# Layer 0's and layer 2's feed forward taken batch by batch, with the normalizations around them, layer 1's k and v projections, and the delta rule's output normalization in its last slots

## The chip, the cores and the metric

The kernel runs on one core of one Trainium2 chip. A core has five engines with instruction queues of their own: PE (matrix multiply, with PEld for its weight loads), DVE (vector), ACT (activation functions and scaled copies), POOL (general vector work), and SP (which here only issues DMAs). Each queue is executed in order; engines wait for each other through semaphores. The metric is the device time of one execution in microseconds; the figure shown is the median of several executions.

## What is computed

A stack of four transformer-like layers on an input x of 4 batches of 1024 tokens with 128 channels, all in float32. Each layer adds two terms to x, both computed from a layer normalization of x. The parts that matter here:

```python
x = x + deltanet(layernorm(x))        # layer 0: a recurrence over tokens; its output o is normalized:
                                      #   (o - mean) / sqrt(var + 1e-5) * ln_w + ln_b
x = x + quantum_ffn(layernorm(x))     # layer 0: h = xn @ W1 + b1
                                      #   q = h + c * sin(theta + 0.1 * h);  relu(q) @ W2 + b2
x = x + ttt(layernorm(x))             # layer 1: k, v = xn @ W_KV, then a sequential scan over tokens
x = x + experts(layernorm(x))
x = x + attention(layernorm(x))       # layer 2
x = x + rwkv_ffn(layernorm(x))        # layer 2: r = sigmoid(xr @ W_r); out = r * (relu(xk @ W_k)^2 @ W_v)
                                      #   xr, xk mix each token with the token before it
x = x + attention(layernorm(x))       # layer 3
x = x + routed_experts(layernorm(x))
```

## The kernel before

x stays on the chip as 32 tiles of 128 tokens (`self.x`), batch b being tiles 8b to 8b+7. A normalization (`layernorm`, which calls `ln_batch` for each of the four batches, lines 92 to 144) takes eight `bn_stats` on DVE (L108), a few small DVE operations (L110 to L114), a square root on ACT (L116), a reciprocal (L117) and a product (L127); then it scales eight tiles, half on ACT (L134) and half on POOL (L132), transposes them on PE (L138) through PSUM, and copies the result into `self.xnT` with ACT (L144). Its pools are opened and closed in `layernorm` itself.

The program is written against a tile framework. Outside of a `manual_schedule` block the framework decides the order of the instructions on each engine: earlier ones in the text have priority, a later one whose inputs are there may pass. Inside a `manual_schedule` block the order of the text holds on each engine. A pool that is opened after another was closed may lie in the same memory, and its first writers then wait for the last readers there. Each pool has a number of buffers (`bufs`) per tile name[...].

**Layer 0's delta rule** (`l0_attn`, lines 174 to 512). 1024 tokens in NS = 32 chunks of 32. The main loop (L441) runs over slots from -LAG-1 to NS+3, LAG being 12, in an order written by hand. In slot c the loop does, among others:

- the state step of chunk c: `up` and `op` (L388), `ux` and `uP` on ACT (L453, L455), `sp` (L464), the state copies (L472), `oT` (L484), `o` (L501) and its store to `od` in DRAM (L502);
- `gram(c + LAG)` (L304, L328): a score whose blocks go to DRAM (`ld`, L331); after every fourth chunk they are read back as `L` (L334);
- `solve(n, i)` (L346, L349), DVE alone: a block of four chunks is solved column by column in eight parts over four slots, two parts a slot, and part 7 stores the result `T` to `td` in DRAM (L351);
- `fetch(c + 2)` (L357): reads chunk c+2's part of T back as `tb`; `apply(c + 1)` (L376) multiplies with it;
- `attend(c + 2)`: a score on PE (L304) and the masked copy `mt` on DVE (L393), which stands between the slot's two solve parts; it shares the PSUM tile `wide` with `gram`;
- `flip(c + LAG + 1)` (L310 to L321): two POOL products and four transposes.

Block n is solved in slots 4n-7 to 4n-4; its first chunk is fetched in slot 4n-2 and applied in slot 4n-1. The output normalization of block n (four chunks) is spread over slots: `reload` in 4n+4 (one DMA from `od`, L408, and a POOL add of the bias, L409), `moments` in 4n+6 (four `bn_stats` and `bn_aggr`, L417 and L418, on DVE), `root` and `norm` in 4n+7 (L423 on ACT; L428, L430 and L432 on DVE).

**Layer 0's feed forward** (`l0_ffn`). After `layernorm()`, 8 chunks of 512 tokens with 4 hidden blocks each: a matmul into `hp` (L559), `r` on ACT (L563), two DVE operations that take off full turns (L530, L531), the sine on ACT (L566), a DVE product (L567), a Relu on ACT (L568); then 16 matmuls into `op` (L573), a POOL add of b2 (L149) and a DVE add to x (L153). The sine of the angles (L549) is one small operation ahead of the chunks.

**Layer 1's attention** (`l1_attn`). After `layernorm()`, for each chunk of 512 tokens a k and a v matmul into `pp` (L619, a PSUM pool of four buffers), copied with a stride of four elements into `kT` by DVE (L621) and into `vT` by ACT (L623). Then `l1_rounds`, a manually ordered sequential scan that begins with chunk 0 of all four batches.

**Layer 2's feed forward** (`l2_ffn`). After `layernorm()`, per batch: two mixes (ACT L1403, DVE L1404), two halves with `kp` (L1408), Relu (L1412), a POOL square (L1413), `rp` (L1417), `vp` (L1422), Sigmoid (L1426), a DVE product (L1427), a POOL add to x (L1429). **Layer 3's attention** (`l3_attn`) begins with `layernorm()` and then `attention`, whose setup (L1092 to L1116) and first projections (L1147) precede its manually ordered main loop.

Of the kernel before, what the change touches and what calls it, by code (L numbers as in the profile page):

```python
# [9 lines left out]
F32 = mybir.dt.float32  # L10
AF = mybir.ActivationFunctionType
# [16 lines left out]
class Net:  # L28
# [71 lines left out]
    def ln_batch(self, pool, ps, b, twice=None):  # L100

# [25 lines left out]
        nc.vector.scalar_tensor_tensor(nm, s, -0.5, rs, ALU.mult, ALU.mult)  # L127
        xn = pool.tile([P, TPB, D], F32, tag="xn", name="xn")
# [39 lines left out]
    def l0_attn(self):  # L168
# [9 lines left out]
        NS, LAG = SEQ // C, 12  # L178
# [3 lines left out]
        with ExitStack() as c_:  # L182
# [222 lines left out]
            def reload(n):  # L405

                o = two.tile([P, NB, D], F32, tag="on", name="on")
                nc.sync.dma_start(o, od[:, n * P : (n + 1) * P, :].rearrange("b p d -> p b d"))  # L408
                nc.gpsimd.tensor_add(of(n), of(n), ln_b.unsqueeze(1).to_broadcast([P, NB, D]))  # L409
                outs[n] = [o]  # L410

            def moments(n):
                o = outs[n][0]
                mv = two.tile([P, NB, 2], F32, tag="mv", name="mv")
# [26 lines left out]
            for slot in range(-LAG - 1, NS + 4):  # L441
                c, part = slot, (slot + 7) % 4
                n = (slot + 7) // 4
# [16 lines left out]
                for i in every(7):  # L460
                    root(i)
# [45 lines left out]
                for i in every(4):  # L507
                    reload(i)
                for i in every(6):
                    moments(i)  # L510
                for i in every(7):
                    norm(i)
# [20 lines left out]
    def l0_ffn(self):  # L533
# [4 lines left out]
        self.layernorm()  # L538
        with tc.tile_pool(name="f0", bufs=3) as two, tc.tile_pool(name="f0c", bufs=1) as one, tc.tile_pool(
            name="f0h", bufs=4, space=PSUM  # L540
        ) as ph, tc.tile_pool(name="f0o", bufs=2, space=PSUM) as po:
            ang = one.tile([P, 3, NF], F32, tag="ang", name="ang")
            nc.vector.tensor_scalar_mul(ang[:, 1, :], f["th"], INV)
            nc.vector.tensor_scalar(ang[:, 2, :], f["th"], INV, 0.25, ALU.mult, ALU.add)
            nc.vector.scalar_tensor_tensor(ang[:, 0, :], f["b1"], 0.1, f["th"], ALU.mult, ALU.add)
            nc.vector.tensor_scalar_mul(ang[:, 0, :], ang[:, 0, :], INV)
            self.turns(one, ang, [P, 3, NF])
            sc = one.tile([P, 2, NF], F32, tag="sc", name="sc")
            nc.scalar.activation(sc, ang[:, 1:3, :], AF.Sin, scale=TWO_PI)  # L549
            co = one.tile([P, NF], F32, tag="co", name="co")  # L550
            nc.vector.tensor_mul(co, sc[:, 1, :], f["wr"])
            nc.vector.tensor_mul(sc[:, 0, :], sc[:, 0, :], f["wi"])
            nc.vector.tensor_add(co, co, sc[:, 0, :])
            nc.vector.scalar_tensor_tensor(co, co, 0.1, f["wi"], ALU.mult, ALU.mult)
            for n in range(NB * SEQ // 512):
# [21 lines left out]
                self.add_four(4 * n, op)  # L577

# [16 lines left out]
    def l1_attn(self):  # L595
# [12 lines left out]
        self.layernorm()  # L608
        with ExitStack() as c_:
            one = c_.enter_context(tc.tile_pool(name="l1c", bufs=1))  # L610
            two = c_.enter_context(tc.tile_pool(name="l1", bufs=2))
            kT = one.tile([P, SEQ, NB], F32, tag="kT", name="kT")
            vT = one.tile([P, SEQ, NB], F32, tag="vT", name="vT")
            with tc.tile_pool(name="l1p", bufs=4, space=PSUM) as ps:
                for n in range(NB * SEQ // 512):
                    b, s = n // 2, (n % 2) * 512
                    for dst, cols in ((kT, slice(0, 128)), (vT, slice(128, 256))):
                        pp = ps.tile([P, 512], F32, tag="pp", name="pp")
                        nc.tensor.matmul(pp, lhsT=wkv[:, cols], rhs=self.tok(4 * n, 512), start=True, stop=True)  # L619
                        if dst is kT:  # L620
                            nc.vector.tensor_copy(dst[:, s : s + 512, b], pp)  # L621
                        else:
# [1084 lines left out]
```

## Time and profile before

| | us |
|---|---|
| median of 3 runs (2716.39 to 2722.8) | 2716.49 |
| the profiled execution, its own time | 2722.97 |
| its span, first to last instruction | 2721.3 |

| engine | busy us | share of the span | instructions |
|---|---|---|---|
| PE | 2465.4 | 91% | 19913 |
| DVE | 1809.7 | 67% | 3643 |
| ACT | 1484.3 | 55% | 3315 |
| POOL | 292.8 | 11% | 526 |

The stages that the change touches, by the times at which their instructions stand in the trace:

| stretch | us from the span's start |
|---|---|
| delta rule: end of the setup, first solve, slot 0, slot 31 | 49.2, 70.0, 112.1, 363.7 |
| last output normalization done, layer 0's first sqrt of the feed forward's normalization | 380.4 |
| first and last work of the eight chunks | 397.5, 474.1 |
| layer 1's normalization done | 490.9 |
| k and v done, layer 1's rounds begin | 508.9 |
| last copy of layer 2's attention | 1507.1 |
| layer 2's feed forward: first mix, last add | 1529.6, 1565.5 |
| layer 3's normalization done, its first projection | 1585.9 |
| first score of layer 3's attention | 1603.8 |

How to read the views: a timeline line has the start and the length in microseconds, the engine, the line of the kernel, the operation, output tile, `<-`, input tiles, shapes, how many were merged, and in brackets how long the engine had been idle and what ended the wait. "SPq" and the like are queue instructions such as DMA issues. A busy share is an average; what bounds a stretch is seen in who waits there.

### The profile page before, as it was taken

Reading aid. Unit: us, or ns where it says so; the run is one execution under the profiler, and the core shown is the slowest. Engines: PE = TensorE matmul, PEld = TensorE weight load, DVE = VectorE, ACT = ScalarE, POOL = GpSimd, SP = SyncE. Lnnn points to the kernel's source line nnn. Section 1 sums busy time; section 2 is a strip of 40 time slices with the busy share of each in tenths; the row PEclk is TensorE's granted clock in tenths of the full one; section 3 lists DMA queues with packets and bytes.
Section 4 is the critical chain, followed back from the end, with each engine's and each line's share of the span. In section 5 each row is a group of like instructions: output and inputs, shape, how many; then the busy total and the mean of one; then the engine's idle time right before and its main releaser. Section 6 shows DMA issues by size and latency. Waiting matters only on the chain.

```text
span 2721.3 us, 50960 instructions
## 1 busy us (share of the span) xinstructions
PE 2465.4 (91%) x19913; PEld 1232.3 (45%) x19913; DVE 1809.7 (67%) x3643; ACT 1484.3 (55%) x3315; POOL 292.8 (11%) x526
## 2 busy tenths in 40 slices
PE   5688758899997989999999669999999999999968
PEld 4455536699995333333333423333333333333356
DVE  5899748566664856776772457767767777777143
ACT  4465457655554424665566523666566666666632
POOL 6112020100002520000000440000000000000011
PEclk8688769899997958999999757999999999999968
DMA  2333220000000001001000000000000000000000
GB/s 47 70 80 78 61 72 1 1 1 1 1 2 2 1 9 17 14 14 18 14 14 5 5 4 6 12 8 9 9 8 8 12 8 9 10 8 8 4 17 17
DMA packets 116718, 46.65 MB, mean 17 GB/s; under 512 B 88473, under 2 KB 111097, under 8 KB 116474
## 3 DMA queue, kind: packets, MB, share of 16 engines
q1 hardware_dynamic: 116474, 43.35, 8.1%
q8 instruction: 159, 2.61, 0.4%
q14 instruction: 85, 0.70, 0.1%
HBM read 17.04 MB, written 12.98 MB: 11 GB/s over the span
## 4 chain that ended last, share of the span: by engine, by line
PE 62%; DVE 4%; ACT 1%; POOL 1%; issue 1%; DMA 0%; SPq 0%; POOLq 0%; DVEq 0%; ACTq 0%
PE pb L1232 31%; PE po L1254 16%; PE pa L1207 5%; PE ep L1026 2%; PE pp L1147 1%; PE tp L138 1%; PE gp L959 1%; PE pv L1128 1%; DVE st L108 1%; PE rp L1625 1%; DVE bm L1219 0%; DVE x L1035 0%; PE bp L1015 0%; PE pr L1480 0%; PE hp L648 0%
## 5 line engine op out<-in xcount | busy, mean ns | idle before, releaser
L1236 ACT ACTIVATE es<-pb 128x512 f32<-128x512 f32 x1536 | 836.2, 594 | 560.0 <-PE pb L1232 405.6
L1232 PE MATMUL pb<-q,k 32*128 32x512 f32 x3072 | 957.8, 642 | 0.9 <-ACT es L1236 0.9
L1207 PE MATMUL pa<-k,q 32*128 32x512 f32 x3072 | 913.4, 682 | 17.2 <-DMA q<-q 15.9
L1219 DVE TENSOR_REDUCE bm<-pa 128x2 f32<-128x1024 f32 x512 | 626.0, 1225 | 276.5 <-PE pb L1232 169.9
L1254 PE MATMUL po<-es,v 128*32 128x256 f32 (+1 forms) x5760 | 480.0, 405 | 0.0
L1232 PEld LDWEIGHTS pb<-q,k 32*128 32x128 f32 x3072 | 314.8, 184 | 348.2 <-ACT es L1236 189.6
L1215 DVE TENSOR_REDUCE bm<-pa 128x16 f32<-128x1024 f32 x256 | 312.8, 1222 | 107.7 <-PE pb L1232 60.7
L1254 PEld LDWEIGHTS po<-es,v 128*32 128x32 f32 x5760 | 114.1, 108 | 543.0 <-issue 510.5
L1207 PEld LDWEIGHTS pa<-k,q 32*128 32x128 f32 x3072 | 254.1, 194 | 94.8 <-DVE bm L1219 50.6
L132 POOL TENSOR_SCALAR xn<-x,rs,nm 128x128 f32<-128x128 f32 x112 | 48.8, 449 | 1259.1 <-DMA oc<-oT 992.5
L138 PE MATMUL tp<-ident,xn 128*128 128x128 f32 x224 | 52.6, 401 | 63.0 <-ACT xn L134 50.3
L346 DVE TENSOR_TENSOR pr<-T,L 128x31 f32<-128x31 f32 (+15 forms) x248 | 90.9, 367 | 27.8 <-DMA L<-ld 20.8
L1261 DVE COPY oT<-po 128x512 f32<-128x512 f32 x48 | 32.7, 682 | 109.1 <-PE po L1254 109.1
L349 DVE TENSOR_TENSOR T<-T,pr 128x31 f32<-128x31 f32 (+15 forms) x248 | 92.8, 374 | 8.5
L304 PE MATMUL wide<-bt,kt 32*128 32x128 f32 x512 | 32.0, 381 | 48.6 <-DVE mt L393 33.3
L138 PEld LDWEIGHTS tp<-ident,xn 128*128 128x128 f32 x224 | 37.7, 196 | 81.2 <-ACT xn L134 45.5
L766 ACT ACTIVATE w<-tr,half 128x128 f32<-128x128 f32 x128 | 47.1, 368 | 48.8 <-PE tr L764 46.7
L741 ACT ACTIVATE a<-hp,wb 128x128 f32<-128x128 f32 x128 | 47.1, 368 | 41.1 <-PE hp L737 40.1
L1026 PE MATMUL ep<-L_ffn_expert_w,xnT 128*128 128x512 f32 x128 | 66.1, 649 | 3.3 <-DVE x L1035 3.0
L464 PE MATMUL sp<-ux,kn 128*128 128x256 f32 x128 | 50.5, 532 | 17.8 <-ACT ux L453 17.7
L749 DVE TENSOR_TENSOR dlt<-gr,mask 128x128 f32<-128x128 f32 x96 | 28.0, 292 | 48.6 <-PE gr L747 48.3
L1035 DVE SCALAR_TENSOR_TENSOR x<-ep,g,x 128x128 f32<-128x128 f32 x160 | 49.5, 342 | 13.1 <-ACT sc L1033 8.1
(462 smaller groups left out, 3466.1 us busy)
## 6 DMA issues: line engine op xcount, KB each, us to landing
ld<-kk SPq DMA_DIRECT2D x128, 32.0 KB
L<-ld SPq DMA_DIRECT2D x8, 512.0 KB
td<-T SPq DMA_DIRECT2D x8, 512.0 KB
tb<-td SPq DMA_DIRECT2D x128, 32.0 KB
md<-nt SPq DMA_DIRECT2D x192, 2.0 KB
q<-md SPq DMA_DIRECT2D x192, 2.0 KB
x<-in_L_attn_x_dram SPq DMA_DIRECT2D x4, 512.0 KB
od<-o SPq DMA_DIRECT2D x32, 64.0 KB
```

Source lines behind the costliest of these rows:

```text
L138: nc.tensor.transpose(tp[:, i, :], xn[:, 4 * n + i, :], self.ident)
L346: nc.vector.tensor_mul(pv, T[:, 0 : j + 1, j : j + 1].to_broadcast(sh), L[:, j : j + 1, j + 1 :].to_broadcast(sh))
L349: nc.vector.tensor_sub(T[:, 0 : j + 1, j + 1 :], T[:, 0 : j + 1, j + 1 :], pv)
L464: mm(sp[:, g].rearrange("p a b -> p (a b)"), lhsT=kns[c % len(kns)][:, 4 * g : 4 * g + 4, :].rearrange("p a b -> p (a b)"), rhs=ux[:, g].r ...
L1026: nc.tensor.matmul(ep.rearrange("p a b -> p (a b)"), lhsT=self.tok(t), rhs=ew[:, 4 * h : 4 * h + 4, :].rearrange("p a b -> p (a b)"), star ...
L1035: nc.vector.scalar_tensor_tensor(xs, eps[e // 4][:, e % 4, :], g[:, e : e + 1], xs, ALU.mult, ALU.add)
L1207: nc.tensor.matmul(pa[:, j % 2, :], lhsT=st["q"][r, i * P : (i + 1) * P], rhs=st["k"][r, n * 512 : (n + 1) * 512], start=True, stop=True,)
L1215: nc.vector.tensor_reduce(out[:, :, 1:9], pa.rearrange("p j (c s) -> p j c s", c=8), axis=AX.X, op=ALU.max)
L1219: nc.vector.tensor_reduce(out[:, :, n : n + 1], pa, axis=AX.X, op=ALU.max)
L1232: nc.tensor.matmul(pb, lhsT=st["k"][r, kc * P : (kc + 1) * P], rhs=st["q"][r, n * 512 : (n + 1) * 512], start=True, stop=True,)
L1236: nc.scalar.activation(es[turn][:, j, :], pb, AF.Exp, scale=scale)
L1254: nc.tensor.matmul(po[r, cols], lhsT=vring[b % 2][:, kc, 4 * g + j, :], rhs=es[:, j, cols], start=kc == 0, stop=True, skip_group_check=True,)
```

## The change

1. `ln_batch` is cut in two: `ln_moments(pool, b)` (up to `rs` and `nm`) and `ln_scale(pool, ps, b, by)` (scaling, transposes, copies). Nothing else of it changes.
2. Delta rule: LAG is 11 instead of 12, the loop runs over 47 slots instead of 49 (-12 to 34), and the solve of block n stands in slots 4n-6 to 4n-3. The output normalization of blocks 0 to 6 is reloaded in slots 23 to 29, one block a slot, that of block 7 in slot 32; moments follow one slot later, root and norm two slots later. The tiles `on` and `mv` have three buffers instead of two.
3. Layer 0's feed forward: all pools are open together; the normalization runs batch by batch between the chunks, and a function handed in by layer 1 (`behind`) normalizes layer 1's input and projects k and v for batches 0 and 1 after chunk 4 and for batches 2 and 3 after chunk 7. The angles' operations stand after the first two batches' scaling. `hp` has three PSUM buffers instead of four, the normalization's `tp` two instead of four, `pp` one instead of four. Layer 1 calls layer 0's feed forward.
4. Layer 2's feed forward: all four moments first, then batch by batch with the scaling one batch ahead; layer 3's normalization of batches 0 and 1 after batch 2, that of batches 2 and 3 after batch 3; `l3_attn` no longer calls `layernorm`. The sigmoid is computed as (tanh(z/2) + 1)/2, the half going into a copy of W_v made once.

```diff
-        NS, LAG = SEQ // C, 12
+        NS, LAG = SEQ // C, 11
...
-            for slot in range(-LAG - 1, NS + 4):
-                c, part = slot, (slot + 7) % 4
-                n = (slot + 7) // 4
+            reloads = [NS - TPB - 1 + i for i in range(TPB - 1)] + [NS]
+            for slot in range(-LAG - 1, NS + 3):
+                c, part = slot, (slot + 6) % 4
+                n = (slot + 6) // 4
...
-                for i in every(7):
-                    root(i)
+                if slot - 2 in reloads:
+                    root(reloads.index(slot - 2))
...
-                for i in every(4):
-                    reload(i)
-                for i in every(6):
-                    moments(i)
-                for i in every(7):
-                    norm(i)
+                if slot in reloads:
+                    reload(reloads.index(slot))
+                if slot - 1 in reloads:
+                    moments(reloads.index(slot - 1))
+                if slot - 2 in reloads:
+                    norm(reloads.index(slot - 2))
```

```diff
-    def l0_ffn(self):
+    def l0_ffn(self, behind):
...
-        self.layernorm()
-        with tc.tile_pool(name="f0", bufs=3) as two, tc.tile_pool(name="f0c", bufs=1) as one, tc.tile_pool(
-            name="f0h", bufs=4, space=PSUM
-        ) as ph, tc.tile_pool(name="f0o", bufs=2, space=PSUM) as po:
+        with ExitStack() as c_:
+            ln = c_.enter_context(tc.tile_pool(name="f0l", bufs=2))
+            few = c_.enter_context(tc.tile_pool(name="f0m", bufs=4))
+            lps = c_.enter_context(tc.tile_pool(name="f0q", bufs=2, space=PSUM))
+            two = c_.enter_context(tc.tile_pool(name="f0", bufs=3))
+            one = c_.enter_context(tc.tile_pool(name="f0c", bufs=1))
+            ph = c_.enter_context(tc.tile_pool(name="f0h", bufs=3, space=PSUM))
+            po = c_.enter_context(tc.tile_pool(name="f0o", bufs=2, space=PSUM))
+            pk = c_.enter_context(tc.tile_pool(name="f0k", bufs=1, space=PSUM))
...
+            pools = few, ln, lps, pk
+            by = [self.ln_moments(few, b) for b in range(2)]
+            for b in range(2):
+                self.ln_scale(ln, lps, b, by[b])
+            angles()
+            chunk(0)
+            chunk(1)
+            by += [self.ln_moments(few, b) for b in range(2, NB)]
+            self.ln_scale(ln, lps, 2, by[2])
+            chunk(2)
+            chunk(3)
+            self.ln_scale(ln, lps, 3, by[3])
+            chunk(4)
+            behind((0, 1), *pools)
+            chunk(5)
+            chunk(6)
+            chunk(7)
+            behind((2, 3), *pools)
...
+            def project(bs, few, ln, lps, ps):
+                by = [self.ln_moments(few, b) for b in bs]
+                for b, m in zip(bs, by):
+                    self.ln_scale(ln, lps, b, m)
+                    for s in range(0, SEQ, 512):
+                        for dst, cols in ((kT, slice(0, 128)), (vT, slice(128, 256))):
+                            pp = ps.tile([P, 512], F32, tag="pp", name="pp")
...
+            self.l0_ffn(project)
             bad = self.l1_rounds(one, kT, vT)
```

```diff
-                            vp[:, i, :], lhsT=ka[:, i * P : (i + 1) * P], rhs=wv, start=True, stop=True
+                            vp[:, i, :], lhsT=ka[:, i * P : (i + 1) * P], rhs=wh, start=True, stop=True
...
-                    nc.scalar.activation(r, rp, AF.Sigmoid)
-                    nc.vector.tensor_mul(r, vp, r)
+                    nc.scalar.activation(r, rp, AF.Tanh, scale=0.5)
+                    nc.vector.scalar_tensor_tensor(r, r, 1.0, vp, ALU.add, ALU.mult)
...
+            by = [self.ln_moments(few, b) for b in range(NB)]
+            for b in range(2):
+                self.ln_scale(ln, lps, b, by[b])
+            batch(0)
+            for b in range(1, NB):
+                if b + 1 < NB:
+                    self.ln_scale(ln, lps, b + 1, by[b + 1])
+                batch(b)
+                if b == 2:
+                    nx = [self.ln_moments(few, i) for i in range(2)]
+                    for i in range(2):
+                        self.ln_scale(ln, lps, i, nx[i])
+            nx = [self.ln_moments(few, i) for i in range(2, NB)]
+            for i in range(2):
+                self.ln_scale(ln, lps, 2 + i, nx[i])
```

## The prediction

> **What bounds the kernel now.** PE is busy for 91% of the span, and the chain of waits runs mostly through the two attentions (L1232, L1254, L1207), which the edit leaves alone. The edit touches three other stretches, each with a limit of its own, so the whole-span shares say nothing about it. I read each stretch by a windows view: per stretch its length, then busy time (and instruction count) of PE, PEld, DVE, ACT, POOL, then granted clock, DMA share, GB/s.
>
> Delta rule, by slots. Slot starts are dated by the one L455 per slot: slot 0 at 112.1, slot 6 at 159.7, slot 20 at 279.3, slot 25 at 317.3, slot 31 at 363.7.
>
> ```profile
> 70.00:112.10 42.10, 19.72 (x204) 13.02 (x204) 38.39 (x104) 12.31 (x25) 1.87 (x3) 0.58 0.23 51
> 112.10:159.70 47.60, 40.40 (x648) 28.36 (x643) 41.88 (x106) 31.01 (x96) 7.72 (x14) 0.90 0.40 93
> 159.70:279.30 119.60, 94.69 (x1520) 67.88 (x1520) 111.99 (x287) 70.85 (x220) 24.18 (x33) 0.87 0.35 77
> 279.30:317.30 38.00, 30.34 (x446) 20.23 (x446) 35.29 (x103) 18.28 (x66) 0.00 (x0) 0.83 0.24 52
> 317.30:363.70 46.40, 36.20 (x514) 25.26 (x514) 15.54 (x43) 20.64 (x75) 0.00 (x0) 0.74 0.20 47
> ```
>
> See the fourth figure: DVE is busy 94% from slot 6 to 20 and its timeline has no hole; it runs without a break from the first solve (70.0) to the last (321.8), then only 33% from slot 25 on. So DVE sets the pace to 321.8. Who pays is in the waits of 112 to 321 us (total, times, longest):
>
> ```profile
> PE wide L304 <- DVE mt L393: 17.9, 9, 4.0
> DVE mt L393 <- PE wide L304: 2.6, 3, 1.4
> ```
>
> Feed forward of layer 0 and layer 1's k and v: all four normalizations, eight chunks, all four normalizations again, the projections.
>
> ```profile
> 380.40:399.70 19.30, 10.58 (x35) 6.44 (x36) 9.38 (x41) 11.99 (x29) 16.93 (x24) 0.50 0.52 133
> 399.70:474.10 74.40, 63.06 (x318) 43.66 (x317) 59.68 (x105) 59.19 (x97) 0.67 (x3) 0.92 0.00 1
> 474.10:490.90 16.80, 7.82 (x32) 5.26 (x32) 9.28 (x63) 12.87 (x29) 7.51 (x20) 0.67 0.00 0
> 490.90:508.90 18.00, 17.10 (x34) 7.44 (x34) 8.84 (x9) 8.57 (x9) 0.00 (x0) 0.84 0.00 1
> ```
>
> The chunks load ACT, DVE and PE alike (80% and more); the pieces around them leave every engine half idle and PE at a clock of 0.50 to 0.84. Layer 2 likewise: normalization, four batches, layer 3's normalization.
>
> ```profile
> 1507.10:1529.60 22.50, 10.53 (x48) 8.62 (x48) 12.14 (x65) 13.28 (x30) 9.49 (x21) 0.58 0.08 13
> 1529.60:1565.50 35.90, 26.69 (x144) 20.42 (x144) 16.50 (x16) 19.00 (x26) 20.23 (x20) 0.84 0.00 0
> 1565.50:1585.90 20.40, 8.06 (x33) 5.64 (x33) 13.89 (x60) 13.10 (x29) 14.17 (x20) 0.57 0.00 0
> ```
>
> **A, the delta rule.** (1) Output normalization. A set is four bn_stats and aggregates (272.96 to 274.65, 1.6 us) and a reciprocal with eight scalar_tensor_tensor (279.90 to 282.58, 2.7 us): 4.3 us of DVE. Five sets (slots 6/7 to 22/23) lie in the saturated stretch; now they go to slots 24 to 31, where DVE is two thirds idle (1.2 + 4.3 us in a 7 us slot). At best 5 x 4.3 = 21.5 us go. Not all: once DVE is relieved, PE and ACT's chain is late next. The nearest row is slots 0 to 6, which hold no set: 47.6/6 = 7.93 us a slot at 88% DVE. Slots 6 to 20 without their four sets are (112.0 - 17.2)/14 = 6.8 us of DVE each, 7.24 at 94% busy, 7.7 at 88%. I take 7.6, nearer the measured slots: 14 x 7.6 = 106 against 119.6, -13. Slots 20 to 25 lose one set, -4.3, held to -3 by the 7 us floor of the last slots. The moved instructions issue as before: eight reload DMAs on SP, which has room in late slots (2.4 us of issue per slot there), and eight 1.4 us POOL adds, where POOL has nothing left to do.
> (2) LAG 11. In the head mt(0) stands behind three solve parts of the second block (93.3 to 104.4); now behind one (4.3 us). PE's slot -1 starts at 105.8 because of it; now the fetched T lets it start at about 100: -6. Against that, T leaves one slot later for the same fetch. Rows of SP and their users:
>
> ```profile
> 93.42 0.34 SPq L351 DMA_DIRECT2D td<-T  x1
> 96.36 1.04 POOL L340 COPY T<-eye 128x1024 f32<-128x1024 f32 x1 [33.31 <-DMA td<-T]
> 321.83 0.35 SPq L351 DMA_DIRECT2D td<-T  x1
> 323.53 2.05 SPq L357 DMA_DIRECT2D tb<-td  x4
> 327.23 1.08 PE L376 MATMUL wp<-tb,vk 128*32 128x128 f32 x16 [2.07 <-DMA tb<-td]
> ```
>
> td lands 2.9 us after issue, four tb issues take 1.9, the last lands 1.65 later: 6.5 us from solve to apply. While DVE leads the pace, PE reaches that apply about 6.6 us after the solve (part 0 and mt 5.5, then 1 to 2 us of PE): no margin. Behind the waiting fetch on SP stand od and the next ld, none of them wanted within a slot. A stall is between 0 and 2 us in each of 7 blocks; I take 0.4, +3. (3) The 10.2 us slot 26 comes from a fetch held on SP behind the last td; in the new order that fetch belongs to the slot before: -3, against +1 for a slot 25 that now solves. The tail after slot 31 (16.7 us: od, on, moments, root, norm) keeps its chain. **Sum A: -13 -3 -6 +3 -3 +1 = -21**; ends -10 (the floor holds all slots at 7.9) and -28.
>
> **B, layer 0's feed forward.** Chunk 0 needs batch 0 alone (last copy 385.7; first ACT of the chunk at 388 instead of 399.7): -11.7. Into the chunks go, on ACT, batches 2 and 3's scaling (2 x 2.8: eight Identity 1.65 per four, two copies 1.16), layer 1's first two (6.2), four v copies of 1.07 (4.3) and about three more table loads: 20 us. ACT there is busy 58.9 of 67.9 us to the last act; at 92%, between that 87% and the 95% of its best slices, (58.9+20)/0.92 = 85.8: +17.9. After the last chunk two normalizations and the projections remain instead of 34.8 us. Two normalizations take 10 us (474.0 to 484.0). The projections have one PSUM bank (bufs=1) instead of four, so matmul (0.9 to 1.7) and strided copy (1.07) alternate: 2.3 to 3.3 each, eight in a row 18 to 26 us. If the scheduler puts batch 2 inside chunk 7, 20 us remain, if not 32.5; I take 27: -7.8. A third hp buffer less (4 to 3): a buffer is held about 4.7 us (0.9+0.7+0.4+0.7+0.6+0.7 and hand-overs), three serve one per 1.6 us where 2.1 is needed: +2. **Sum B: about 0**, ends -8 and +8.
>
> Two rules speak against B. Trainium skill, "ScalarE: Activation LUTs", section "Table sets: the hidden batching unit": call functions of one set together; sin, sqrt, sin, sqrt is the opposite. Its section on the load's cost gives 1.28 us and a drain, 2.66 together. The trace:
>
> ```profile
> 402.19 0.69 ACT L563 ACTIVATE r<-hp,ang 128x512 f32<-128x512 f32 x1 [0.17 <-PE hp L559]
> 402.90 1.28 ACT L566 ACT_TABLE_LOAD   x1
> 404.19 1.67 ACT L566 ACTIVATE s<-r 128x512 f32<-128x512 f32 x3
> ```
>
> 1.3 us from end to start. Three more loads are 3.9 us by the row, 8 by the rule; the row decides. Second, "SBUF — State Buffer": a DVE instruction with two SBUF inputs and a GpSimd one that reads SBUF exclude each other for their whole length. Here:
>
> ```profile
> 1573.80 4.71 DVE L110 TENSOR_TENSOR d<-st 128x8 f32<-128x8 f32 x1
> 1573.84 4.64 POOL L1460 TENSOR_TENSOR x<-x,L_attn_out_b 128x1024 f32<-128x1024 f32 x2
> ```
>
> A 0.17 us op held for 4.7: agreed. In B some 17 us of POOL (xn, b2 adds) now meet L531's 22 us of DVE in 86; a quarter colliding is 4 us on DVE, which has slack (60+10 of 86): 0, and +4 if that slack is gone. In A it is why slots with reloads stretch, which leave.
>
> **C, layer 2.** Batch 0 needs two normalizations (copies done 1522.8, not 1529.6): -6.8. The FFN stretch takes in four scalings: PE 26.7+7.9, ACT 19+11+2.6 (two loads), POOL 20.2+7. PE alone fills 34.6 of 35.9, so it cannot be free: +5, ends 0 and +11. Tanh instead of Sigmoid and one fused DVE op are the same count; nothing. Layer 3's normalization keeps two batches: 10.3 us (1565.5 to 1575.8) of 20.4: -10.1. The 17.9 us of attention setup behind it stay. **Sum C: -12**, ends -17 and -4.
>
> **Total.** -33 on the profiled execution's 2722.97 (span 2721.3) is 2690; it stands 6.5 above the median 2716.49, so about 2684. No change means within 0.3%, 8.1 us.
>
> **Rivals.** *The gaps fill* (0.15): batch 2 vanishes into the chunks, A and C reach their good ends: -28-8-17, 2663. For it: 87% ACT. Against: one PSUM bank. *The floor* (0.22): slots stay near 7.9, the single bank and the extra loads lengthen the tail, the text's order is undone by the scheduler, which already pulls L549's sine ahead of L423: -10+5-6 = -11, 2705. For it: slots 0 to 6. *T late* (0.07): the fetch behind its own td stalls every block. Price s for 7 blocks; from s = 4.7 us it eats 33 us, at 6 us the time is 2726. For it: no margin computed above. Against: 6.5 us measured. *No net effect* 0.06, forecast 0.50 (own range 2673 to 2696). Range for 8 in 10: 2664 to 2706. Faster 0.87, same 0.06, slower 0.07.
>
> **What would show it.** A: slots 6 to 20 at 7.6 us, DVE near 90% until slot 25, no DMA wait on L376 over 2 us; wrong if slots stay at 8.5 or L376 waits each fourth slot. B: first chunk 12 us earlier after the last norm, layer 1's rounds starting as far from it as now (128 us). C: from the last oT copy of layer 2 to layer 3's first project 67 us instead of 79. Wrong altogether if the attentions change length.

## The result and the profile after

| | before | after |
|---|---|---|
| median of 11 runs each, us | 2716.49 | 2708.41 |
| lowest and highest | 2712.07 to 2722.8 | 2703.23 to 2714.49 |
| ratio after/before (95%) | | 0.997 (0.9958 to 0.9982) |
| profiled execution's own time; its span | 2722.97; 2721.3 | 2712.38; 2710.7 |

The change gains 8 us, not the 33 of the forecast, and the time lies above my range. The first step is to cut both traces at the same events and see in which stage the profiled 10.6 us are. All in us; "predicted" is the sum of my steps.

| stage, from event to event | before | after | difference | predicted |
|---|---|---|---|---|
| start to the delta rule's slot 0 | 112.1 | 106.5 | -5.6 | -6 |
| slot 0 to slot 6 | 47.6 | 48.1 | +0.5 | 0 |
| slot 6 to 20 | 119.6 | 111.8 | -7.8 | -13 (and +3 for a late T) |
| slot 20 to 25 | 38.0 | 41.9 | +3.9 | -3 |
| slot 25 to 31 | 46.4 | 47.1 | +0.7 | -2 |
| slot 31 to the last output norm | 16.6 | 16.1 | -0.5 | 0 |
| **A, the sum of these** | 380.3 | 371.5 | **-8.8** | -21 |
| last norm to the first scaled chunk | 19.4 | 11.4 | -8.0 | -11.7 |
| that to the last x add of the chunks | 73.7 | 100.7 | +27.0 | +19.9 |
| that to layer 1's first round | 35.5 | 21.0 | -14.5 | -7.8 |
| **B** | 128.6 | 133.0 | **+4.4** | 0 |
| layer 1's rounds and layer 2's attention | 998.2 | 995.7 | -2.5 | 0 |
| last oT copy to layer 2's first mix | 22.4 | 15.6 | -6.8 | -6.8 |
| first mix to the last x add of its feed forward | 35.9 | 55.7 | +19.8 | +5 |
| that to layer 3's first projection | 20.4 | 5.6 | -14.8 | -10.1 |
| **C** | 78.8 | 76.9 | **-1.9** | -12 |
| the rest | 1135.4 | 1133.5 | -1.9 | 0 |

Helper lines have moved: L455 is L466 now, L393 L402, L340 L349, L409 L418, L559 L579, L619 L659. The windows view of the kernel after, delta rule (length, then busy time and count of PE, PEld, DVE, ACT, POOL, clock, DMA share, GB/s):

```profile
154.60:253.40 98.80, 81.37 (x1400) 57.68 (x1400) 87.07 (x217) 65.39 (x202) 15.46 (x29) 0.95 0.36 82
253.40:277.90 24.50, 16.43 (x214) 11.35 (x214) 20.39 (x31) 9.91 (x31) 10.13 (x8) 0.72 0.23 50
308.30:355.40 47.10, 34.88 (x514) 24.01 (x514) 37.77 (x138) 21.51 (x81) 0.00 (x0) 0.78 0.28 69
```

The first row is slots 6 to 18: 98.8/13 = 7.6 us each, with DVE at 88%, as forecast. The second row is slots 19 and 20 alone: 24.5 us, where 15.2 would do. That row holds 9.3 us more than it should, and its POOL column is odd: eight instructions, 10.1 us. The third is where the normalizations went; DVE has room for them.

The two feed forwards, same view:

```profile
382.90:484.30 101.40, 79.99 (x376) 51.74 (x374) 77.80 (x171) 87.31 (x146) 15.85 (x25) 0.92 0.04 9
484.30:504.50 20.20, 11.90 (x23) 4.13 (x23) 4.95 (x16) 8.41 (x12) 3.01 (x10) 0.68 0.00 0
1515.90:1571.60 55.70, 36.15 (x182) 26.56 (x182) 28.77 (x71) 38.83 (x64) 34.23 (x39) 0.80 0.00 1
1571.60:1577.20 5.60, 1.98 (x9) 1.42 (x9) 1.82 (x11) 3.12 (x7) 3.03 (x5) 0.50 0.00 0
```

In both, what follows the batches is shorter (by 14.6 and 14.8 us), but the batches took in more than that (27.0 and 19.8). The busiest engine is ACT in both, 86% in the first and 70% in the second. So waits hold them as well as work, and the experiments have to say which.

### The profile page after: what moved, and what is told of

Same layout as the page of the kernel before. It is cut to its first block, busy times and chain, and to the rows that moved or that the text cites. A ratio compares the mean times of both kernels' runs of the same rounds, so it can differ in the third digit from the quotient of the medians.

```text
span 2710.7 us, 50997 instructions
## 1 busy us (share of the span) xinstructions
PE 2459.9 (91%) x19913; PEld 1222.5 (45%) x19913; DVE 1813.6 (67%) x3644; ACT 1494.8 (55%) x3327; POOL 293.2 (11%) x525
## 4 chain that ended last, share of the span: by engine, by line
PE 63%; DVE 3%; ACT 1%; POOL 1%; issue 1%; SPq 0%; DMA 0%; POOLq 0%; DVEq 0%; ACTq 0%
PE pb L1276 31%; PE po L1298 16%; PE pa L1251 5%; PE ep L1070 2%; PE pp L1191 1%; PE tp L147 1%; PE gp L1003 1%; PE pv L1172 1%; PE rp L1692 1%; DVE bm L1263 0%; DVE x L1079 0%; PE bp L1059 0%; PE pr L1547 0%; PE hp L692 0%; DVE k L1147 0%
## 5 line engine op out<-in xcount | busy, mean ns | idle before, releaser
L355 DVE TENSOR_TENSOR pr<-T,L 128x31 f32<-128x31 f32 (+15 forms) x248 | 93.2, 376 | 28.0 <-DMA L<-ld 20.7
L147 PE MATMUL tp<-ident,xn 128*128 128x128 f32 x224 | 46.8, 356 | 46.7 <-ACT xn L143 41.5
L810 ACT ACTIVATE w<-tr,half 128x128 f32<-128x128 f32 x128 | 47.0, 367 | 49.1 <-PE tr L808 46.4
```

The costliest lines, as they stand in the source:

```text
L147: nc.tensor.transpose(tp[:, i, :], xn[:, 4 * n + i, :], self.ident)
L355: nc.vector.tensor_mul(pv, T[:, 0 : j + 1, j : j + 1].to_broadcast(sh), L[:, j : j + 1, j + 1 :].to_broadcast(sh))
```

## Experiments

The middle of the program (rounds and layer 2's attention, about 996 us) is the same in all kernels, yet its length in the profiled executions ran from 992.9 to 1000.7 us with PE busy between 958 and 969. A few us of any total are that. The verdicts below rest on stage lengths first, on medians second. Stages with the same text vary too: A ends at 359.6 to 364.4 in the six kernels that gate the adds and are else as changed there, at 368.2 to 371.5 in the five without the gate. Each ratio is against runs of the kernel before on the same chip. B ends at the first `hp` matmul of layer 1's rounds.

| run | median | ratio to before (95%) | A ends at | B | C |
|---|---|---|---|---|---|
| before | 2716.49 | 1 | 380.3 | 128.6 | 78.8 |
| after | 2708.41 | 0.997 (0.9958 to 0.9982) | 371.5 | 133.0 | 76.9 |
| gated adds | 2699.21 | 0.9948 (0.9933 to 0.9963) | 359.6 | 133.3 | 77.7 |
| no root loads | 2712.66 | 0.999 (0.9977 to 1.0004) | 370.4 | 135.6 | 76.9 |
| batch 3 first | 2709.87 | 0.9983 (0.9972 to 0.9993) | 370.4 | 133.5 | 73.0 |
| all three | 2705.14 | 0.9969 (0.9958 to 0.998) | 359.7 | 137.1 | 72.7 |
| shared ring | 2696.79 | 0.9939 (0.9925 to 0.9954) | 368.8 | 118.5 | 77.8 |
| ring, layer 1 behind | 2684.62 | 0.9898 (0.9881 to 0.9915) | 368.2 | 109.8 | 77.8 |
| lag alone | 2719.31 | 1.002 (1.0009 to 1.0032) | 376.1 | 133.9 | 78.1 |
| delta rule alone, gated | 2693.33 | 0.9925 (0.9912 to 0.9939) | 364.4 | 122.1 | 79.5 |
| best, batch 3 first | 2678.81 | 0.9855 (0.9838 to 0.9871) | 363.9 | 110.4 | 73.0 |
| best, layer 3's LN behind | 2680.52 | 0.9864 (0.9847 to 0.9881) | 360.8 | 110.4 | 72.0 |
| four hidden buffers, one bank | 2699.36 | 0.993 (0.9914 to 0.9946) | 363.0 | 128.2 | 78.1 |
| best, root one later | 2674.54 | 0.9841 (0.982 to 0.9863) | 362.0 | 110.6 | 72.7 |

### The delta rule: the eight adds

The timeline of the kernel after at slot 19 (start, duration, engine, line, operation):

```profile
251.71 1.04 POOL L349 COPY T<-eye 128x1024 f32<-128x1024 f32 x1 [9.73 <-DVE pr L355]
252.71 10.83 POOL L418 TENSOR_TENSOR x<-x,L_attn_ln_b 128x512 f32<-128x512 f32 x8
256.99 1.31 DVE L358 TENSOR_TENSOR T<-T,pr 128x192 f32<-128x192 f32 x1
258.33 1.33 DVE L355 TENSOR_TENSOR pr<-T,L 128x207 f32<-128x207 f32 x1
263.81 0.40 DVE L355 TENSOR_TENSOR pr<-T,L 128x231 f32<-128x231 f32 x1
```

The text places each add with its reload, in slots 23 to 29 and 32. But an add needs only x and the bias, both there long since, and after the last copy of the identity nothing else stands in POOL's queue. So POOL runs all eight in one row, from 252.7 to 263.5, beside a solve that DVE bounds. Seven of the eight solve instructions of DVE beside them then take as long as one add (1.3 us), and 0.4 us again once the adds are over. `mt`, one of whose inputs lies in PSUM, takes 1.21 us among the adds and 1.22 behind them. Seven times 0.95 us too much are 6.7 of the 9.3 us. Slot 20, which starts behind the last add, pays through DVE's backlog. PE waits for `mt` late in both slots (us in total, times, longest):

```profile
PE wide L313 <- DVE mt L402: 8.1, 2, 4.6
```

The kernel before shows the same on a smaller scale:

```profile
260.68 4.07 POOL L409 TENSOR_TENSOR x<-x,L_attn_ln_b 128x512 f32<-128x512 f32 x3
```

Its text has these three adds in slots 24, 28 and 32. They ran in one row at the start of slot 18, the longest of that loop (11.6 us).

The first experiment makes the adds wait for a copy of the bias:

```diff
 def reload(n):
-    nc.gpsimd.tensor_add(of(n), of(n), ln_b.unsqueeze(1).to_broadcast([P, NB, D]))
 def moments(n):
+    lb = two.tile([P, D], F32, tag="lb", name="lb")
+    nc.scalar.copy(lb, ln_b)
+    nc.gpsimd.tensor_add(of(n), of(n), lb.unsqueeze(1).to_broadcast([P, NB, D]))
```

> The changed kernel, except that each reload's GpSimd bias add reads a copy of the bias that ScalarE makes one slot after the reload, so that no add can run before slot 24. Theory (the eight adds, run in one row of 10.8 us beside the solve in slots 19 and 20, hold up DVE's two-input instructions): slots 19 and 20 fall from 12.9 and 11.5 us to about 7.6 each, less 0 to 2 us for three adds that still meet the last solve; 7 to 9 us less than the changed kernel, 2699 to 2702. Rival (the adds are bystanders; slots 19 and 20 are long because of the lower clock there, 0.72, or the last T's fetch): slots 19 and 20 keep 11 us or more and the time stays at 2708.

Slots 19 and 20 took 8.3 and 7.3 us; A ends at 359.6, 11.9 us earlier than after the change. The timeline of this kernel, the same solve and the first add:

```profile
252.99 0.36 DVE L358 TENSOR_TENSOR T<-T,pr 128x192 f32<-128x192 f32 x1
253.38 0.37 DVE L355 TENSOR_TENSOR pr<-T,L 128x207 f32<-128x207 f32 x1
295.99 1.34 POOL L423 TENSOR_TENSOR x<-x,lb 128x512 f32<-128x512 f32 x1 [45.36 <-ACT lb L422]
```

The same two instructions, 0.36 us for 1.31 and 0.37 for 1.33. POOL waits 45 us at the gate, which costs nobody anything. The windows view of the two slots in this kernel:

```profile
251.30:266.90 15.60, 11.46 (x214) 8.27 (x214) 13.75 (x30) 9.62 (x31) 0.00 (x0) 1.00 0.23 41
```

The granted clock went from 0.72 to 1.00. The edit touches no matmul, so the low clock came with the stall and was not its cause. The effect repeats: slots 19 and 20 together took 23.8 to 24.5 us in the five kernels that have the moved adds without the gate, and 15.6 to 16.4 us in the seven with it. By the ratios the gain is 0.2% (6 us; the two intervals still overlap a little), by the stage 11.9, and 8 in the mean of the kernels with this text. The theory holds.

The second question is whether the moved sets made the slots shorter at all, or the lag of 11:

```diff
-if slot in reloads:
-    reload(reloads.index(slot))
+for i in every(4):
+    reload(i)
...
+for i in every(6):
+    moments(i)
+for i in every(7):
+    norm(i)
```

> The changed kernel with the delta rule's output normalizations back in their old slots (one set every four slots); only the lag of 11 is left of the change there. Theory (the sets of 4.3 us of DVE in the DVE-bound slots made the 0.9 us a slot): slot 0 stays at about 106, slots 6 to 20 take 8.3 to 8.6 us each as before the change, the last normalization ends at 373 to 377, and the time is 2 to 5 us above the changed kernel. Rival (the lag, not the moved sets, makes the slots shorter): slots 6 to 20 take 7.6 to 7.9 us, and since the adds are spread too, the last normalization ends at 360 to 365, 8 us or more below the changed kernel.

Slot 0 starts at 105.5, so the head's 6 us are the lag's. Slots 6 to 20 took (276.8 - 154.5)/14 = 8.7 us, a little above the forecast: the moved sets, with their adds, are what shortened them. Slot 19 took 13.9 us of it; the last three adds stand there in one row. A ends at 376.1, inside the theory's range; the time was above it (1.002 against 0.997, about 14 us), of which the stage shows 4.6 and the untouched middle 4.5.

> The kernel before with the delta rule's part of the change alone, its GpSimd adds gated as in the first experiment; both feed forwards as before. Theory (the delta rule with gated adds is worth 20.7 us, layer 0's feed forward costs 4.4, layer 2's saves 2.8): 19 to 22 us below the kernel before, that is within 3 us of the first experiment's or better. Rival (the two feed forwards earn their place once nothing else holds them back): 6 us or more above the first experiment.

The edit is the delta rule's part of the change, with the gate, on the kernel before. It gives 0.9925, 20 us less than before, as expected. It is not worse than the same delta rule with both new feed forwards (0.9948): as they stand in the change, they earn nothing. One caution: layer 0's chunks, with the same instructions as before, took 66.7 us here and 73.7 before, at a granted clock of 0.99 and 0.92. PE, ACT and DVE have their instructions in another order there in the two builds; I haven't separated that from the clock. So a comparison with the 73.7 us of the kernel before can be off by 7 us.

The last wait of A was found in slot 26, which still takes 9.7 us after the change although the fetch I blamed has moved. The timeline of the kernel after:

```profile
318.68 0.35 SPq L360 DMA_DIRECT2D td<-T  x1
320.24 0.30 ACT L432 ACTIVATE rs<-mv,eps 128x4 f32<-128x4 f32 x1 [3.88 <-DVE mv L427]
320.45 1.08 ACT L483 COPY S<-sp 16x128 f32<-16x128 f32 x4
```

ACT stands 3.9 us at a root whose moments stand on DVE behind the last solve, and the state copies queue behind the root. Root and norm one slot later, with four buffers for the reloaded outputs and their moments and one more slot in the loop, on the best version below:

```diff
-if slot - 2 in reloads:
-    root(reloads.index(slot - 2))
+if slot - 3 in reloads:
+    root(reloads.index(slot - 3))
...
-if slot - 2 in reloads:
-    norm(reloads.index(slot - 2))
+if slot - 3 in reloads:
+    norm(reloads.index(slot - 3))
```

> The best version so far (gate, ring with layer 1 behind, fourth batch first) with the root and the norm of each output set one slot later, and one buffer more for each. Theory (slot 26 stays 10 us long because ScalarE stands 3.4 to 4.8 us at a root whose moments stand on DVE behind the last solve, and the state copies queue behind it): no wait of ScalarE for moments over 1 us in slots 25 to 27, slot 26 falls from 10.7 us to 7 to 8, the last output normalization ends at 359 to 361 instead of 363.9, and the time is 2 to 4 us lower, 2675 to 2677. Rival (slot 26 is long because of the last T's fetch): slot 26 keeps 10 us, and the time does not move.

Slot 26 fell to 5.8 us, and slot 27 took 13.4. The waits and the timeline of this kernel:

```profile
PE wp L385 <- DMA tb<-td: 5.7, 1, 5.7
311.96 0.35 SPq L360 DMA_DIRECT2D td<-T  x1
314.99 1.79 SPq L366 DMA_DIRECT2D tb<-td  x4
```

With the root out of the way PE reaches the fetch of the last T before it has landed, and waits 5.7 us for it. ACT still waited 2.3 us for moments in slot 27, where the theory had no wait over 1. Slots 25 to 27 took 25.8 us against 27.7, and A ends 1.9 us earlier, less than the 3 to 5 expected: both were late, the root first. Theory and rival each hold half. A gain is not shown: another kernel with the early root ends A at 360.8, this one at 362.0, and the two totals can't be told apart (0.9841 and 0.9855).

### Layer 0's feed forward

The trace after has 12 table loads between the last output norm and layer 1's rounds, ten of them inside the chunks (12.8 us of ACT); the kernel before has four for the same functions, two of them ahead of the last norm. I had counted three more. That was the first suspect. The edit, where mh is -0.5:

```diff
-nc.scalar.activation(rs, q, AF.Sqrt, bias=self.eps, scale=1.0 / D)
-nc.vector.reciprocal(rs, rs)
+nc.vector.tensor_scalar(q, q, 1.0 / D, EPS, ALU.mult, ALU.add)
+nc.gpsimd.tensor_tensor(rs, q, self.mh.to_broadcast([P, TPB]), ALU.pow)
```

> The changed kernel, except that the eight normalizations in and around layer 0's feed forward take (variance + eps)^-0.5 with one DVE multiply-add and one small GpSimd power instead of ScalarE's Sqrt and DVE's reciprocal: no table is swapped between Sin and Sqrt. Theory (the ten added table loads, 12.8 us of ScalarE in a stretch where it is 86% busy, are what I under-counted): from the first scaled chunk to the last x add 101 us fall to 89 to 93, and the time falls by 8 to 12 us, to about 2698. Rival (PE, three hp buffers and the single projection bank set the stretch's pace): the loads go and the stretch loses no more than 3 us, 2705 to 2708.

The loads went, and with them 10.5 us of ACT in the stretch (87.3 to 76.9); the stretch lost 2.5 us (100.7 to 98.2). The start grew by 4.2: the power instruction took 1.65 us for 8 elements a partition and stands in front of POOL's scaling. PE's waits in the stretch, first of the kernel after, then of this one:

```profile
PE hp L579 <- DVE s L587: 17.1, 6, 5.7
```

```profile
PE tp L152 <- ACT xn L148: 11.2, 5, 4.7
PE hp L584 <- DVE s L592: 5.0, 4, 2.9
```

A wait of the same size took the place of the one removed: PE's queue now stops at transposes whose input isn't scaled yet. The outcome is the rival's, but its cause is not shown by this run. The windows view of the stretch here:

```profile
386.10:485.00 98.90, 78.38 (x379) 50.22 (x377) 78.73 (x173) 76.85 (x132) 27.16 (x30) 0.94 0.01 1
```

POOL's time rose from 15.9 to 27.2 us, and its powers stand ahead of the scaling that PE now waits for. So the run shows what this replacement brings; what the loads alone cost stays open. I had forecast ACT as the limit at 92%; with 10.5 us of it gone, the stretch is 2.5 us shorter.

> The changed kernel, except that layer 0's hidden tiles and layer 1's k and v projections share one ring of four PSUM buffers instead of three and one. Theory (the stretch is long because PE waits 17.1 us for a hidden buffer that DVE still reads, and the tail because the single projection bank makes matmul and copy alternate): from the first scaled chunk to the last x add 101 us fall to 90 to 94, the tail from 21 to 16 to 18; 9 to 14 us less than the changed kernel. Rival (PE's 80 us of matmuls now stand in one order with transposes that wait for ScalarE and GpSimd, and buffers are not it): the stretch stays at 98 or more, the tail loses at most 4 us.

```diff
-ph = c_.enter_context(tc.tile_pool(name="f0h", bufs=3, space=PSUM))
-pk = c_.enter_context(tc.tile_pool(name="f0k", bufs=1, space=PSUM))
+ph = c_.enter_context(tc.tile_pool(name="f0h", bufs=4, space=PSUM))
...
-pools = few, ln, lps, pk
+pools = few, ln, lps, ph
...
-pp = ps.tile([P, 512], F32, tag="pp", name="pp")
+pp = ps.tile([P, 512], F32, tag="hp", name="pp")
```

B fell from 133.0 to 118.5: the stretch from 100.7 to 96.4, the tail from 21.0 to 10.7. The tail of the kernel after, and the same projections with the ring:

```profile
495.76 1.12 PE L659 MATMUL pp<-xnT,L_attn_W_KV 128*128 128x512 f32 x2 [1.15 <-DVE kT L663]
496.93 1.05 ACT L665 COPY vT<-pp 128x512 f32<-128x512 f32 x1 [3.58 <-PE pp L659]
498.03 1.58 PE L659 MATMUL pp<-xnT,L_attn_W_KV 128*128 128x512 f32 x2 [1.14 <-ACT vT L665]
```

```profile
477.60 3.70 PE L658 MATMUL pp<-xnT,L_attn_W_KV 128*128 128x512 f32 x8
```

With one bank (one PSUM buffer), matmul and copy take turns, 2.3 to 2.7 us a projection; with the ring four projections are 3.7 us of PE. One run tells the two buffers apart. It has the gated adds, and the fourth hidden buffer is taken from the transposes:

```diff
-lps = c_.enter_context(tc.tile_pool(name="f0q", bufs=2, space=PSUM))
+lps = c_.enter_context(tc.tile_pool(name="f0q", bufs=1, space=PSUM))
...
-ph = c_.enter_context(tc.tile_pool(name="f0h", bufs=3, space=PSUM))
+ph = c_.enter_context(tc.tile_pool(name="f0h", bufs=4, space=PSUM))
```

> The changed kernel with gated adds, four hidden buffers in PSUM instead of three, one bank for the normalizations' transposes instead of two, and the single projection bank kept. It tells apart what the ring brought. If the single projection bank is the cost (theory): from the last x add to layer 1's rounds 20 to 22 us as in the changed kernel, against 11 with the ring. If the third hidden buffer less is the cost of the chunks: the stretch is 95 to 97 us as with the ring, not 101. If neither: both stay, and the ring's gain came from another order.

The stretch was 97.4, the tail 19.9. So the fourth hidden buffer is worth 3 to 4 us in the chunks, the projections' banks 9 to 10 in the tail. In total the ring gains 0.3% (8 us) by the ratios, a little less than expected, and 14.5 us by the stage; the stretch stayed above the theory's 94, the tail fell below its 16.

> As the shared ring, and layer 1's batches 0 and 1 are normalized and projected behind chunk 7, with batches 2 and 3, instead of behind chunk 4. Theory (17 us of PE work put into a stretch that had PE at 85% costs about what it saves behind it): the stretch falls to 80 to 88 us, the tail grows to 30 to 36; all of it, from the last output normalization to layer 1's rounds, within 3 us of the shared ring's run. Rival (the chunks do hide layer 1's first two batches): all of it is 6 us or more longer than the shared ring's.

```diff
 chunk(4)
-behind((0, 1), *pools)
 chunk(5)
 chunk(6)
 chunk(7)
+behind((0, 1), *pools)
 behind((2, 3), *pools)
```

The stretch fell to 81.8, the tail grew to 16.6. The first `hp` matmul of layer 1's rounds with the shared ring, and here:

```profile
487.31 0.39 PE L780 MATMUL hp<-kT,wb 128*128 128x128 f32 x2
```

```profile
477.96 0.39 PE L780 MATMUL hp<-kT,wb 128*128 128x128 f32 x2
```

B is 109.8, 8.7 us less than with layer 1's first two batches inside the chunks. There they cost 14.6 us of stretch and save 5.9 behind it: more than they save, which neither theory nor rival had. Three later kernels with the same text in this stage had B at 110.4, 110.4 and 110.6, so the gain repeats. In the trace the first of the four batches is still projected inside the last chunk, where the scheduler puts it; that may be why the tail grew so little. The time fell by 0.4% (11 us); in the profiled executions 8.7 of 11.3 are this stage.

### Layer 2's feed forward

The timeline after, around its fourth batch:

```profile
1538.79 0.57 ACT L153 COPY xnT<-tp 128x512 f32<-128x512 f32 x1
1552.50 4.64 POOL L1527 TENSOR_TENSOR x<-x,L_attn_out_b 128x1024 f32<-128x1024 f32 x2
1554.15 2.19 ACT L1455 ACTIVATE m<-xnT,mi 128x1023 f32<-128x1023 f32 x2
1555.34 2.89 DVE L1456 SCALAR_TENSOR_TENSOR m<-xnT,L_ffn_mu_r,m 128x1024 f32<-128x1024 f32 x1 [3.20 <-ACT m L1455]
1558.28 2.93 PE L1469 MATMUL rp<-L_ffn_W_rT,m 128*128 128x128 f32 x12 [4.65 <-DVE m L1456]
```

The fourth batch's input is complete at 1539.4; its first mixing starts at 1554.2, since layer 3's first two normalizations stand ahead of it in the text and on ACT. Then DVE's mixing takes 2.9 us for 1.3, beside POOL's bias add (layer 3's, drawn forward), and PE waits 4.65 us.

> The changed kernel, except that layer 2's fourth batch is issued ahead of layer 3's normalization of batches 0 and 1 instead of behind it. Theory (in the changed kernel the fourth batch's mixing starts 15 us after its normalized input is there, because ScalarE, GpSimd and the 4.6 us of layer 3's bias adds stand ahead of it; PE idles 4.7 us): from the last copy of layer 2's attention to layer 3's first projection 77 us become 68 to 72, and the time falls by 5 to 9 us, to 2700 to 2703. Rival (the work only changes places: what comes off the batches is added to the normalization behind them): within 2 us of the changed kernel's 2708.

```diff
                 batch(b)
-                if b == 2:
-                    nx = [self.ln_moments(few, i) for i in range(2)]
-                    for i in range(2):
-                        self.ln_scale(ln, lps, i, nx[i])
+            nx = [self.ln_moments(few, i) for i in range(2)]
+            for i in range(2):
+                self.ln_scale(ln, lps, i, nx[i])
```

The stretch fell by 8.0 us (55.7 to 47.7), and 4.1 came back behind it (5.6 to 9.7): C is 73.0, 3.9 us less. In the median nothing is seen (0.9983), so the size rests on the stage alone. It repeats: C is 72.7 to 73.0 in the four kernels with this order, 76.9 to 78.1 in the seven with that of the change.

> The three edits together (gated bias adds, no Sqrt in layer 0's feed forward, layer 2's fourth batch first). The stages are 100 us and more apart, so if each theory holds the gains add: 20 to 30 us below the changed kernel, about 2684. If one of the rivals holds, its share is missing here too; if the stages are not independent, the sum of the three single gains differs from this one by over 3 us.

The gate and the batch order each showed the same stage gain as alone (A ends at 359.7, C 72.7), B was 137.1; the time was 2705.1 where about 2684 was expected. Of the 21 us short, 8 to 12 are the gain of the missing loads that didn't come, 4 the power instruction's cost, 5 the untouched middle, the longest of all runs (1000.7).

### Together

Both runs carry the gate, the ring and layer 1 behind the chunks:

> Gated adds, the shared ring with layer 1 behind the chunks, and layer 2's fourth batch ahead of layer 3's first normalizations, all on the changed kernel. Theory (the three stages are apart, so the stage gains add): the last output normalization ends at about 360, layer 1's rounds start 115 to 119 us after it, layer 3's first projection stands 73 us after layer 2's last attention copy; 9 to 12 us from the gate and 2 to 4 from the batch order below the ring's 2684.6 (of a before of 2713): 2669 to 2675, 38 to 44 us below the kernel before. Rival (part of the ring's gain was a chance of the scheduler's order, which another kernel doesn't repeat): the stage of layer 0's feed forward is back at 120 us or more, and the time over 2680.

> As the run beside it (gate, ring, layer 1 behind), but all four of layer 3's normalizations stand behind layer 2's batches, as before the change; only batch 0's early start and the interleaved scalings of layer 2 remain. Theory (interleaving layer 3's normalization lengthens the batches by about as much as it saves behind them): from layer 2's last attention copy to layer 3's first projection 72 to 77 us, within 3 us of the run beside it. Rival (the interleaving earns what I gave it, 10 us): 80 us or more.

```diff
-            nx = [self.ln_moments(few, i) for i in range(2)]
-            for i in range(2):
-                self.ln_scale(ln, lps, i, nx[i])
-            nx = [self.ln_moments(few, i) for i in range(2, NB)]
-            for i in range(2):
-                self.ln_scale(ln, lps, 2 + i, nx[i])
+            nx = [self.ln_moments(few, i) for i in range(NB)]
+            for i in range(NB):
+                self.ln_scale(ln, lps, i, nx[i])
```

The first gives 0.9855, 39 us less than the kernel before and 31 less than the change. The 39 us are inside the theory's 38 to 44; the 2678.8 us lie above its 2669 to 2675, which it reckoned from a kernel before of 2713, and here that took 2717.8. A ended at 363.9 instead of 360. B is 110.4 in both runs, below the theory's 115 to 119, a range that dates the first round by a later matmul. That is 18 us below the kernel before, and the ring's gain holds up. The edit shown is the second run's. It has C at 72.0 for 73.0, so how layer 3's normalization is laid out behind the batches doesn't matter. In both runs all of it stands behind them in the text, so the pair does not test the interleaving that its expectation names; that it costs 4 us ahead of the fourth batch, as in the change, is shown by the run above. With the later root the best median is 2674.54.

## Why the prediction was wrong

Of the 33 us, A misses 12, C 10 and B 4; another 4 came from stages that the edit leaves alone, which is luck.

**A, the lag and the slots: right.** Head -5.6 for -6; slots 6 to 18 at 7.60 for 7.6; PE's waits for the fetched T are at most 1.5 us each. With the gate A is -20.7 for -21, in part by luck: the +3 for a late T did not come, and slots 20 to 31 gave 0.7 instead of 5. Five other kernels with the gate have -16.0 to -20.6.

**A, the moved instructions: the step that failed.** I wrote "eight 1.4 us POOL adds, where POOL has nothing left to do". Count and duration were right, the place was not: I put the adds where the text has them. Nothing held them there; POOL, idle, ran them 4 to 13 slots earlier, beside a solve on DVE that sets the pace. The rule for what this costs was in my own text (the Trainium skill, "SBUF — State Buffer", section "Who interferes with whom": a DVE instruction with two inputs in SBUF contends with a GpSimd one that reads SBUF; here 0.36 us became 1.31), and I said for A that slots with reloads "leave". They came back in one row. That is 9.3 us in slots 19 and 20, 11.9 up to the last norm. The three adds in slot 18 of the kernel before, 6 to 14 slots ahead of their text, showed it beforehand; I hadn't followed them.

**A, slot 26: wrong.** I gave -3 for the fetch that is no longer behind the last td, and +1 for a slot 25 that solves. Slots 25 to 31 took +0.7: behind the fetch, ACT's root was late next, and behind the root the fetch again.

**B: mechanism half right, sizes off in three terms that partly cancel.** First chunk -8.0 for -11.7: the first root stands 2.7 us behind the last norm, for 0.1 before, and on ACT the second batch's scaling, a load and the angles stand in front of the chunk. The stretch +27.0 for +19.9: I worked it out from ACT's busy time, and the runs show other terms. Layer 1's first two batches, 10.5 us of ACT or 11.4 at my 92%, took 14.6 us of the stretch with the ring and gave back 5.9 behind it. The third buffer less was priced at 2, for which my sum gave no reason (one buffer per 1.6 us where one per 2.1 is needed), and is 3 to 4. The tail -14.5 for -7.8: batch 2's normalization and its first projection did run inside chunk 7, the case of 20 us that I had averaged with another, and they are part of the longer stretch. The single bank was priced rightly and is 9 to 10 us of the tail. The added loads were eight, not three; taking all of them away, with powers on POOL in their place, brought 2.5 us.

**C: the start right, the batches wrong.** -6.8 as forecast. The stretch was +19.8 for +5: I summed busy times and did not follow the order of the text, in which the fourth batch stands behind layer 3's normalization. Behind it -14.8 for -10.1. The order is worth 3.9 of the 10 us that C is short. ACT has six table loads in the stretch for one before, where I had added two; no run takes them away, and the rest stays open.

**Rivals.** The gain of 8.08 us is just inside "no net effect" (8.1). "The floor" (2705) is 3 us off, and its stages come near (-10, +5 and -6 for -8.8, +4.4 and -1.9), but by luck in A: slots 6 to 18 did not stay at 7.9. Its single bank was right; what its extra loads cost stays open. "T late" did not happen, except in slot 27 of the run with the later root.

## What to carry to other kernels

An instruction runs as soon as its operands are there and its queue is free, not where the text has it: when an edit moves work later, ask what keeps it late. On an idle engine the answer may be "nothing", and if it shares something with the bounding engine, gate it by data that is made late. The trace of the kernel before may show it already: compare where an instruction ran with where its text stands. And when a stage is 80% full on three engines, more work put into it is not hidden (here 14.6 us in for 5.9 saved behind it): follow each queue's order and each ring of buffers, not the busy shares.

## What the runs showed of the hardware

GpSimd's power of 128x8 values took 1.65 us, longer than its add of 128x512 (1.26 to 1.35). Eight adds in a row held seven of DVE's solve instructions to 1.3 us, where they take 0.3 to 0.4 alone: one add, one DVE instruction, in turn. It need not be in turn: in the row that the prediction shows, one DVE instruction was held for two adds (4.71 us for 0.17). And the granted clock rose from 0.72 to 1.00 in the two slots whose stall was removed; the same 214 matmuls took 16.4 us of PE with the stall and 11.5 without.
